# Layer 0 of a graph and feed-forward network: the adjacency product as two float32r products instead of one float32 product

## The chip, the cores and the metric

The kernel runs on one core of one Trainium2 chip. The metric is the time of one execution on the device, in microseconds (us); lower is better. Times given as a median come from runs without a profile. Everything said about where time goes comes from one further execution, which the hardware profiler recorded.

## The reference

There are 32 graphs of 512 nodes with 256 features. Layer 0 is a graph convolution and a feed-forward block, each added to its input after a layer norm; layer 1 is a graph attention and a slice mixer and is not touched by the change. The graph convolution, which the change concerns, is:

```python
a = adj.astype(x.dtype)                       # [32, 512, 512], ones and zeros
h = jnp.einsum('bnf,fu->bnu', x, W_msg)       # messages; x is the normed input
msg_sum = jnp.einsum('bij,biu->bju', a, h)    # sum over the neighbours
deg = jnp.sum(a, axis=1)
messages = jnp.where(deg[..., None] > 0, msg_sum / jnp.maximum(deg, 1.0)[..., None], 0.0)
out = jnp.einsum('bnf,fu->bnu', x, W_upd) + messages + bias
return jax.nn.relu(out)
```

The feed-forward block has two dense branches of 1024 columns (a gelu and a gate) and a tropical branch, the maximum over features of `x + Wt`, followed by piecewise linear functions; the branches are mixed and multiplied by `Wd`. All arithmetic is in float32.

## The kernel before

`layer0_sorted` does layer 0. A graph has 512 rows, four tiles of 128. The graph convolutions run graph by graph. The feed-forward runs over 32 groups of 512 rows that have been put in another order, so that rows needing many lookups in the tropical branch share a tile; the graphs are ordered in four segments of eight.

The convolution of a graph has two generators. `conv_in` loads x and the adjacency (`adji`, int32), casts the adjacency to floating point on GpSimd (line 392), norms x and transposes it to `x1T` (`layer_norm_T`, line 33), and computes the messages `h` (line 403) in two PSUM tiles `ph`, each copied to SBUF by ScalarE (line 405). Column 256 of `h` is set to one by a GpSimd memset (line 397), so that the product with the adjacency yields the degree as well. `conv_out` computes x times `W_upd` (`pu`, line 421), adds the bias into `u` (line 424), and multiplies adjacency by messages (`pm`, line 430): for each of four row tiles, four products of 128 rows are accumulated over 257 columns. VectorE divides by the degree and adds (lines 433 to 435), applies the relu and the residual into `keep` (line 438), norms the result again (lines 441 to 452), looks for its eight greatest values (lines 455 to 457), and ScalarE counts values above a bound (line 460). `rows_of` receives `keep` by DMA. `put_in_order` sorts a segment when its eight graphs are done.

The feed-forward has `sums`, which gathers rows and table entries by indirect DMA on GpSimd's queue (lines 549, 560 and 591) and takes maxima on VectorE (line 594), `mixed`, which does the two dense products (`clsp` and `gatep`, line 619), their activations on ScalarE (line 621), transposes of the tropical values (`tz`, line 626) and the piecewise functions and mixing on VectorE (`acc`, lines 633 to 637), and `down`, which multiplies by `wd` (`po`, line 648) and adds the result into the rows (line 650).

These are generators, woven in a fixed ratio: first the first segment's convolutions with the preparation of the weights (`features`), then the feed-forward groups with the remaining convolutions, and after the last convolution with the beginning of layer 1. The engines' instruction orders are then set by a planner, which places instructions by estimated times and by priority within the order in which they were written, so a change of an operation can move its neighbours. [...]

Buffers: the tag `mm` is a pair of PSUM tiles that `ph`, `pu`, `pm` and `po` use in turn. In SBUF the pool `sa` holds the convolution's tiles; `h` has one buffer, so the memset of the next graph's `h` waits until the last `pm` of this one has read it. The tag `ln_xn` holds normed tiles, in three buffers.

Of the kernel before, what the change touches and what calls it, by code (L numbers as in the profile page):

```python
# [7 lines left out]

F32 = mybir.dt.float32
I32 = mybir.dt.int32  # L10
BF16 = mybir.dt.bfloat16
U32 = mybir.dt.uint32
# [6 lines left out]
P = 128  # L19
N = 512  # L20
D = 256
NT = N // P
# [10 lines left out]
def layer_norm_T(nc, sb, ps, ident, eps, x, xnT, name, kept=None, pool=False):  # L33


    mv = sb.tile([P, NT, 2], F32, tag="ln_mv", name=f"mv{name}", bufs=2)
    for t in range(NT):
        st = sb.tile([P, 6], F32, tag="ln_st", name=f"st{name}_{t}", bufs=4)
        nc.vector.bn_stats(st, x[:, t, :])
        nc.vector.bn_aggr(mv[:, t, :], st)  # L40
    rs = sb.tile([P, NT], F32, tag="ln_rs", name=f"rs{name}", bufs=2)
    if pool:
        deviation(nc, rs, mv[:, :, 1], eps)
        shift = sb.tile([P, NT], F32, tag="ln_shift", name=f"shift{name}", bufs=2)
        nc.vector.scalar_tensor_tensor(shift, mv[:, :, 0], -1.0, rs, ALU.mult, ALU.mult)
    else:
        nc.scalar.activation(rs, mv[:, :, 1], AF.Sqrt, bias=eps[:, 0:1])
        nc.vector.reciprocal(rs, rs)
    pt = [ps.tile([P, NT, P], F32, tag="tp", name=f"lnp{name}_{c}") for c in range(DC)]
    for t in range(NT):  # L50
        if kept is None:
            xn = sb.tile([P, D], F32, tag="ln_xn", name=f"xn{name}_{t}", bufs=3)
        else:
            xn = kept[:, t, :]
        if pool:
            nc.scalar.activation(xn, x[:, t, :], AF.Identity, bias=shift[:, t : t + 1], scale=rs[:, t : t + 1])
        else:
            nc.vector.tensor_scalar(xn, x[:, t, :], mv[:, t, 0:1], rs[:, t : t + 1], ALU.subtract, ALU.mult)
        for c in range(DC):
            nc.tensor.transpose(pt[c][:, t, :], xn[:, c * P : (c + 1) * P], ident)  # L60
    for c in range(DC):
        nc.scalar.copy(xnT[:, c, :], pt[c].rearrange("p t n -> p (t n)"))
# [34 lines left out]
def layer0_sorted(tc, ident, eps, x, adj, w, x2s, ranks, over, following):  # L97
# [29 lines left out]
    with ExitStack() as ctx:  # L127
# [30 lines left out]
        for i, cap in enumerate(CAPS):  # L158
            if i == 0 or cap != CAPS[i - 1]:
                nc.gpsimd.memset(limits[:, i:], 2.0 * cap + 1.0 - D)  # L160
        count_to = cst.tile([P, P], I32, tag="count_to", name="count_to")
        nc.gpsimd.iota(count_to, pattern=[[1, P]], base=0, channel_multiplier=0)
        upto = cst.tile([P, P], BF16, tag="upto", name="upto")
        nc.vector.tensor_copy(upto, count_to)
        nc.gpsimd.iota(count_to[:, 0:1], pattern=[[0, 1]], base=0, channel_multiplier=1)
        own_part = cst.tile([P, 1], F32, tag="own_part", name="own_part")
        nc.vector.tensor_copy(own_part, count_to[:, 0:1])

        CT = NC * ST
        below = cst.tile([P, CT // P, CT], BF16, tag="below", name="below")  # L170
# [213 lines left out]
        def conv_in(b):  # L384

            xg = sa.tile([P, NT, D], F32, tag="x", name=f"x{b}")
            nc.sync.dma_start(xg, x[b].rearrange("(t p) d -> p t d", p=P))
            a = sa.tile([P, NT, N], F32, tag="adj", name=f"adj{b}", bufs=2)
            for t in range(NT):
                ai = sa.tile([P, N], I32, tag="adji", name=f"adji{b}_{t}", bufs=2)  # L390
                nc.sync.dma_start(ai, adj[b, t * P : (t + 1) * P, :])
                nc.gpsimd.tensor_copy(a[:, t, :], ai)
            x1T = sa.tile([P, DC, N], F32, tag="x1T", name=f"x1T{b}", bufs=2)
            layer_norm_T(nc, sa, ps, ident, eps, xg, x1T, f"a{b}", pool=True)
            yield
            h = sa.tile([P, NT, D + 1], F32, tag="h", name=f"h{b}", bufs=1)
            nc.gpsimd.memset(h[:, :, D : D + 1], 1.0)
            for t0 in range(0, NT, 2):
                ph = ps.tile([P, 2, D], F32, tag="mm", name=f"ph{b}_{t0}")
                for i in range(2):  # L400
                    t = t0 + i
                    for c in range(DC):
                        nc.tensor.matmul(ph[:, i, :], x1T[:, c, t * P : (t + 1) * P], w_msg[:, c, :],
                                         start=c == 0, stop=c == DC - 1)
                nc.scalar.copy(h[:, t0 : t0 + 2, :D], ph)  # L405
            held[b] = xg, a, x1T, h
            yield

        def conv_out(b, counts):


            xg, a, x1T, h = held.pop(b)
            keep = sa.tile([P, NT, RW], F32, tag="keep", name=f"keep{b}")
            mv = sa.tile([P, NT, 2], F32, tag="mv", name=f"mv{b}")
            for t0 in range(0, NT, 2):
                two = slice(t0, t0 + 2)
                pu = ps.tile([P, 2, D], F32, tag="mm", name=f"pu{b}_{t0}")
                for k in range(2):
                    t = t0 + k
                    for c in range(DC):  # L420
                        nc.tensor.matmul(pu[:, k, :], x1T[:, c, t * P : (t + 1) * P], w_upd[:, c, :],
                                         start=c == 0, stop=c == DC - 1)
                u = sa.tile([P, 2, D], F32, tag="upd", name=f"u{b}_{t0}", bufs=1)
                nc.vector.tensor_add(u, pu, bias.unsqueeze(1).to_broadcast([P, 2, D]))
                deg = sa.tile([P, 2], F32, tag="deg", name=f"deg{b}_{t0}")
                for k in range(2):
                    t = t0 + k
                    pm = ps.tile([P, N], F32, tag="mm", name=f"pm{b}_{t}")
                    for i in range(NT):
                        nc.tensor.matmul(pm[:, : D + 1], a[:, i, t * P : (t + 1) * P], h[:, i, :],  # L430
                                         start=i == 0, stop=i == NT - 1)

                    nc.vector.tensor_scalar_max(deg[:, k : k + 1], pm[:, D : D + 1], 1.0)
                    nc.vector.reciprocal(deg[:, k : k + 1], deg[:, k : k + 1])
                    nc.vector.scalar_tensor_tensor(u[:, k, :], pm[:, :D], deg[:, k : k + 1], u[:, k, :],  # L435
                                                   ALU.mult, ALU.add)
                    yield
                nc.vector.scalar_tensor_tensor(keep[:, two, :D], u, 0.0, xg[:, two, :], ALU.max, ALU.add)
                for t in range(t0, t0 + 2):
                    st = sa.tile([P, 6], F32, tag="ln_st", name=f"stb{b}_{t}", bufs=4)  # L440
                    nc.vector.bn_stats(st, keep[:, t, :D])
                    nc.vector.bn_aggr(mv[:, t, :], st)
            rs = sa.tile([P, NT], F32, tag="ln_rs", name=f"rsb{b}", bufs=2)
            deviation(nc, rs, mv[:, :, 1], eps)
            shift = sa.tile([P, NT], F32, tag="ln_shift", name=f"shiftb{b}", bufs=2)
            nc.vector.scalar_tensor_tensor(shift, mv[:, :, 0], -1.0, rs, ALU.mult, ALU.mult)
            for t in range(NT):
                k, n = keep[:, t, :], b * NT + t
                nc.gpsimd.tensor_copy(k[:, MEAN : MEAN + 1], shift[:, t : t + 1])
                nc.gpsimd.tensor_copy(k[:, MEAN + 1 : MEAN + 2], rs[:, t : t + 1])  # L450
                xn = sa.tile([P, D], F32, tag="ln_xn", name=f"xnb{b}_{t}", bufs=3)
                nc.scalar.activation(xn, k[:, :D], AF.Identity, bias=shift[:, t : t + 1], scale=rs[:, t : t + 1])
                rest = sa.tile([P, D], F32, tag="rest", name=f"rest{n}")
                bound = ends[:, 0, n : n + 1]
                nc.vector.tensor_tensor_reduce(rest, xn, low, -1.0, 3e38, ALU.add, ALU.min, bound)
                nc.vector.max(k[:, VAL : VAL + 8], xn)
                nc.vector.max_index(k[:, IDX : IDX + 8].bitcast(U32), k[:, VAL : VAL + 8], xn)


                nc.scalar.activation(rest, xn, AF.Sign, bias=bound, accum_out=counts[:, t : t + 1])  # L460
                nc.gpsimd.tensor_copy(k[:, COUNT : COUNT + 1], counts[:, t : t + 1])
                nc.gpsimd.tensor_copy(ends[:, 1, n : n + 1], k[:, VAL : VAL + 1])
                if t + 1 < NT:
                    yield
            rows = rows_of[b // SEG].rearrange("(b t p) w -> b p t w", t=NT, p=P)
            nc.sync.dma_start(rows[b % SEG], keep)
            yield
# [1767 lines left out]
```

## Time and profile before

| what | value |
|---|---|
| median of three runs | 4594.69 us (4590.96 to 4598.55) |
| profiled execution, first to last instruction | 4609.8 us |
| TensorE, VectorE, ScalarE, GpSimd busy | 89%, 73%, 50%, 37% of the span |
| first and last `pm` product | 32.1 us and 1875.4 us |
| first and last `clsp` product | 325.9 us and 2483.1 us |
| mean granted TensorE clock | 0.952 of full speed |

The only time known of the profiled execution is its span; it is 15.1 us (0.3%) longer than the median of the runs without a profile, and no time outside it is recorded. A line such as "L430 PE MATMUL pm<-h,adj" names the line of the kernel, the engine (PE is TensorE, PEld its weight loads, DVE VectorE, ACT ScalarE, POOL GpSimd, SP the queue that issues most DMAs), the operation, and the tiles written and read. Recorded ends of matmuls are modelled, and a record's length includes a drain that the next one overlaps; so the distance between starts, not the length, is what a matmul costs in a row of them. The idle time of an engine is put down to whatever ended it last.

### The profile page before, as it was taken

Reading aid. Unit: us, or ns where it says so; the run is one execution under the profiler, and the core shown is the slowest. Engines: PE = TensorE matmul, PEld = TensorE weight load, DVE = VectorE, ACT = ScalarE, POOL = GpSimd, SP = SyncE. Lnnn points to the kernel's source line nnn. Section 1 sums busy time; section 2 is a strip of 40 time slices with the busy share of each in tenths; the row PEclk is TensorE's granted clock in tenths of the full one; section 3 lists DMA queues with packets and bytes.
Section 4 is the critical chain, followed back from the end, with each engine's and each line's share of the span. In section 5 each row is a group of like instructions: output and inputs, shape, how many; then the busy total and the mean of one; then the engine's idle time right before and its main releaser. Section 6 shows DMA issues by size and latency. Waiting matters only on the chain.

```text
span 4609.8 us, 56079 instructions
## 1 busy us (share of the span) xinstructions
PE 4083.4 (89%) x19287; PEld 2519.8 (55%) x19287; DVE 3357.7 (73%) x6944; ACT 2291.2 (50%) x4756; POOL 1726.9 (37%) x2036
## 2 busy tenths in 40 slices
PE   5767898989989899879897999999999999999997
PEld 4544555656556566545554355555555555555555
DVE  6668777877788877776675777767777777777763
ACT  2344565545655555545564444545444455454433
POOL 2356544654537444353332332222323333222220
PEclk8888999999999999998998999999999999999998
DMA  5556533654437543374431111111111111111100
GB/s 131 162 162 203 172 122 120 202 180 139 141 95 226 168 133 126 97 254 143 137 115 48 53 47 56 54 40 46 46 49 56 56 53 56 46 56 56 40 14 15
DMA packets 235100, 474.09 MB, mean 103 GB/s; under 512 B 38299, under 2 KB 114075, under 8 KB 234804
## 3 DMA queue, kind: packets, MB, share of 16 engines
q0 software_dynamic: 80256, 282.38, 19.1%
q1 hardware_dynamic: 154548, 188.02, 13.3%
q8 instruction: 154, 2.52, 0.2%
q14 instruction: 142, 1.16, 0.1%
HBM read 413.16 MB, written 57.16 MB: 102 GB/s over the span
## 4 chain that ended last, share of the span: by engine, by line
PE 33%; DVE 30%; DMA 11%; POOL 11%; issue 10%; ACT 5%; SPq 0%; DVEq 0%; POOLq 0%; ACTq 0%
DVE att L1209 5%; PE clsp L619 4%; PE gatep L619 4%; PE avp L1242 3%; PE pm L430 3%; DVE acc L633 3%; DMA rows<-table,xs 2%; PE po L648 2%; DVE sw L1332 2%; DVE best L594 2%; PE yTp L1342 2%; DMA rows<-table,tops 2%; DVE sw L1337 2%; PE adp L1249 2%; DVE sst L1335 2%
## 5 line engine op out<-in xcount | busy, mean ns | idle before, releaser
L619 PE MATMUL clsp<-xnT,wc 128*128 128x512 f32 x1024 | 522.8, 629 | 74.0 <-ACT cls L621 57.5
L619 PE MATMUL gatep<-xnT,wg 128*128 128x512 f32 x1024 | 501.6, 608 | 6.8 <-ACT gate L621 5.9
L648 PE MATMUL po<-wd,acc 128*128 128x256 f32 x2048 | 455.1, 382 | 4.9 <-ACT h L405 3.0
L1209 DVE SCALAR_TENSOR_TENSOR att<-own,other,mask 128x512 f32<-128x512 f32 x512 | 392.1, 790 | 75.4 <-DMA own<-ownd 75.4
L648 PEld LDWEIGHTS po<-wd,acc 128*128 128x128 f32 x2048 | 390.5, 192 | 71.5 <-issue 13.0
L430 PE MATMUL pm<-h,adj 128*128 128x257 f32 x1024 | 292.4, 431 | 121.5 <-DVE u L435 46.9
L633 DVE SCALAR_TENSOR_TENSOR acc<-past,fld,acc 128x512 f32<-128x512 f32 x448 | 347.6, 778 | 57.9 <-ACT past L632 47.6
L594 DVE SCALAR_TENSOR_TENSOR best<-rows,xs,best 128x1024 f32<-128x1024 f32 x212 | 274.2, 1296 | 152.6 <-ACT best L588 90.1
L628 ACT ACTIVATE acc<-tz,fld 128x512 f32<-128x512 f32 x256 | 198.6, 776 | 283.6 <-PE tz L626 283.5
L591 POOL DMA_INDIRECT rows<-table,xs x212 | 254.4, 1200 | 218.0 <-DVE best L594 159.5
L619 PEld LDWEIGHTS gatep<-xnT,wg 128*128 128x128 f32 x1024 | 197.5, 196 | 251.6 <-issue 206.3
L632 ACT ACTIVATE past<-tz,fld 128x512 f32<-128x512 f32 x448 | 290.6, 691 | 79.2 <-DVE acc L633 78.8
L619 PEld LDWEIGHTS clsp<-xnT,wc 128*128 128x128 f32 x1024 | 187.6, 201 | 224.5 <-issue 121.2
L430 PEld LDWEIGHTS pm<-h,adj 128*128 128x128 f32 x1024 | 210.2, 216 | 181.4 <-issue 103.0
L1242 PE MATMUL avp<-att,hv 128*64 128x512 f32 x1024 | 304.8, 617 | 2.3 <-DVE att L1209 2.3
L1342 PE MATMUL yTp<-sw,x 128*128 128x512 f32 x512 | 256.2, 636 | 56.9 <-DVE sw L1337 54.0
L621 ACT ACTIVATE cls<-clsp,fld 128x512 f32<-128x512 f32 x256 | 175.1, 684 | 205.5 <-PE clsp L619 97.3
L1295 POOL TENSOR_TENSOR mu<-mu,eps 128x16 f32<-128x16 f32 x32 | 112.9, 3527 | 381.1 <-DVE mu L1294 381.0
L1330 PE MATMUL lgp<-wsl,x4T 128*128 128x512 f32 x512 | 244.3, 611 | 11.0 <-ACT sw L1331 3.7
L1150 POOL DMA_INDIRECT x<-x2s,ranks x128 | 136.2, 1064 | 296.8 <-DVE att L1209 133.1
L621 ACT ACTIVATE gate<-gatep,fld 128x512 f32<-128x512 f32 x256 | 175.3, 685 | 141.4 <-PE gatep L619 113.3
L549 POOL DMA_INDIRECT xs<-rows_of,order x128 | 145.1, 1133 | 228.7 <-DVE acc L633 62.6
(598 smaller groups left out, 8944.3 us busy)
## 6 DMA issues: line engine op xcount, KB each, us to landing
adji<-in_adj SPq DMA_DIRECT2D x128, 256.0 KB
ai<-in_adj SPq DMA_DIRECT2D x128, 256.0 KB
own<-ownd SPq DMA_DIRECT2D x128, 256.0 KB
rows_of<-keep SPq DMA_DIRECT2D x32, 550.0 KB
x<-in_x SPq DMA_DIRECT2D x32, 512.0 KB
x2s<-xs SPq DMA_DIRECT2D x32, 512.0 KB
out<-x SPq DMA_DIRECT2D x32, 512.0 KB
rows<-table,xs POOLq DMA_INDIRECT x212
```

The source lines that it names most:

```text
L430: nc.tensor.matmul(pm[:, : D + 1], a[:, i, t * P : (t + 1) * P], h[:, i, :], start=i == 0, stop=i == NT - 1)
L591: nc.gpsimd.indirect_dma_start(out=row, out_offset=None, in_=table, in_offset=bass.IndirectOffsetOnAxis(ap=idxs[:, k : k + 1].bitcast(U32) ...
L594: nc.vector.scalar_tensor_tensor(m, row, vals[:, k : k + 1], m, ALU.add, ALU.max)
L619: nc.tensor.matmul(pf, wf[:, c, f * P : (f + 1) * P], xnT[:, c, :], start=c == 0, stop=c == DC - 1)
L621: nc.scalar.activation(o, pf, fn, bias=fld[:, f, bf : bf + 1], scale=1.0 if fn == AF.Gelu else 0.5)
L632: nc.scalar.activation(r, z, AF.Relu, bias=fld[:, f, AT + b : AT + b + 1])
L633: nc.vector.scalar_tensor_tensor(y, r, fld[:, f, CH + b : CH + b + 1], y, ALU.mult, ALU.add)
L648: nc.tensor.matmul(po[:, i, :], acc[f][:, t * P : (t + 1) * P], wd[:, f, :], start=f == 0, stop=f == FC - 1)
L1209: nc.vector.scalar_tensor_tensor(e, own[h], other[:, j, h : h + 1], mask[:, j, :], ALU.max, ALU.mult)
L1242: nc.tensor.matmul(pv[q][k * HO : (k + 1) * HO, :], hv[:, j, h, :HO], weighed[b, h, j], start=j == 0, stop=j == NT - 1)
L1330: nc.tensor.matmul(pf, xnT[:, c, t * P : (t + 1) * P], wsl[:, c, :], start=c == 0, stop=c == DC - 1)
L1342: nc.tensor.matmul(py, xn[:, t, c * P : (c + 1) * P], sw[:, t, :], start=t == 0, stop=t == NT - 1)
```

## The change

The product of adjacency and messages is done in float32r instead of float32, twice: once with the messages as ScalarE rounds them on writing a float32r tile (`high`), and once with what the rounding left (`low_half`), which VectorE computes by a subtraction from the PSUM tile. Both are accumulated in the same PSUM tile. The messages tile `h` grows from 257 to 514 columns: 256 of the high half, two of ones, 256 of the low half. The adjacency is cast to float32r.

The rest makes room in SBUF for the larger tile. `u` is no longer a tile of its own but the first 256 columns of `keep`; the tile `rest`, whose elements nobody reads, becomes bf16; the tag `ln_xn` gets two buffers instead of three; and `count_to`, used only at the start, is given back after use, by a pool on the side where the convolution's pool is then placed.

```diff
     for t in range(NT):
         if kept is None:
-            xn = sb.tile([P, D], F32, tag="ln_xn", name=f"xn{name}_{t}", bufs=3)
+            xn = sb.tile([P, D], F32, tag="ln_xn", name=f"xn{name}_{t}", bufs=2 if pool else 3)
...
-        count_to = cst.tile([P, P], I32, tag="count_to", name="count_to")
-        nc.gpsimd.iota(count_to, pattern=[[1, P]], base=0, channel_multiplier=0)
         upto = cst.tile([P, P], BF16, tag="upto", name="upto")
...
+        with tc.tile_pool(name="count", bufs=1, side="right") as counting:
+            count_to = counting.tile([P, P], I32, tag="count_to", name="count_to")
+            nc.gpsimd.iota(count_to, pattern=[[1, P]], base=0, channel_multiplier=0)
+            nc.vector.tensor_copy(upto, count_to)
...
-            a = sa.tile([P, NT, N], F32, tag="adj", name=f"adj{b}", bufs=2)
+            a = sa.tile([P, NT, N], F32R, tag="adj", name=f"adj{b}", bufs=2)
...
-            h = sa.tile([P, NT, D + 1], F32, tag="h", name=f"h{b}", bufs=1)
-            nc.gpsimd.memset(h[:, :, D : D + 1], 1.0)
+            h = sa.tile([P, NT, 2 * D + 2], F32R, tag="h", name=f"h{b}", bufs=1)
+            nc.gpsimd.memset(h[:, :, D : D + 2].bitcast(F32), 1.0)
...
-                nc.scalar.copy(h[:, t0 : t0 + 2, :D], ph)
+                high, low_half = h[:, t0 : t0 + 2, :D], h[:, t0 : t0 + 2, D + 2 :]
+                nc.scalar.copy(high, ph)
+                nc.vector.tensor_sub(low_half, ph, high.bitcast(F32))
...
-                u = sa.tile([P, 2, D], F32, tag="upd", name=f"u{b}_{t0}", bufs=1)
+                u = keep[:, two, :D]
...
                     for i in range(NT):
-                        nc.tensor.matmul(pm[:, : D + 1], a[:, i, t * P : (t + 1) * P], h[:, i, :],
-                                         start=i == 0, stop=i == NT - 1)
+                        for c0, c1 in ((0, D + 2), (D + 2, 2 * D + 2)):
+                            nc.tensor.matmul(pm[:, : c1 - c0], a[:, i, t * P : (t + 1) * P], h[:, i, c0:c1],
+                                             start=i + c0 == 0, stop=i + 1 == NT and c0 > 0)
...
-                xn = sa.tile([P, D], F32, tag="ln_xn", name=f"xnb{b}_{t}", bufs=3)
+                xn = sa.tile([P, D], F32, tag="ln_xn", name=f"xnb{b}_{t}", bufs=2)
...
-                rest = sa.tile([P, D], F32, tag="rest", name=f"rest{n}")
+                rest = sa.tile([P, D], BF16, tag="rest", name=f"rest{n}")
```

More of the change, by code (lines that the diff above doesn't have):

```diff
@@ L9 @@
 F32 = mybir.dt.float32
+F32R = mybir.dt.float32r
 I32 = mybir.dt.int32
@@ L160, in layer0_sorted @@
                 nc.gpsimd.memset(limits[:, i:], 2.0 * cap + 1.0 - D)
-        count_to = cst.tile([P, P], I32, tag="count_to", name="count_to")
-        nc.gpsimd.iota(count_to, pattern=[[1, P]], base=0, channel_multiplier=0)
         upto = cst.tile([P, P], BF16, tag="upto", name="upto")
-        nc.vector.tensor_copy(upto, count_to)
-        nc.gpsimd.iota(count_to[:, 0:1], pattern=[[0, 1]], base=0, channel_multiplier=1)
         own_part = cst.tile([P, 1], F32, tag="own_part", name="own_part")
-        nc.vector.tensor_copy(own_part, count_to[:, 0:1])
+        with tc.tile_pool(name="count", bufs=1, side="right") as counting:
+            count_to = counting.tile([P, P], I32, tag="count_to", name="count_to")
+            nc.gpsimd.iota(count_to, pattern=[[1, P]], base=0, channel_multiplier=0)
+            nc.vector.tensor_copy(upto, count_to)
+            nc.gpsimd.iota(count_to[:, 0:1], pattern=[[0, 1]], base=0, channel_multiplier=1)
+            nc.vector.tensor_copy(own_part, count_to[:, 0:1])
         CT = NC * ST
```

## The prediction

> **What bounds the kernel now.** I read the page's busy shares first, then the busy time by stretch, then the chain for the part that the change touches, then the waits and durations around line 430, the product of adjacency and messages.
>
> The page, sections 1, 4 and 5 (busy time and share; the chain by engine; the group: count, busy us, mean ns, idle time before it):
> ```profile
> PE 4083.4 (89%) x19287; PEld 2519.8 (55%) x19287; DVE 3357.7 (73%) x6944; ACT 2291.2 (50%) x4756; POOL 1726.9 (37%) x2036
> ...
> PE 33%; DVE 30%; DMA 11%; POOL 11%; issue 10%; ACT 5%; SPq 0%; DVEq 0%; POOLq 0%; ACTq 0%
> ...
> L430 PE MATMUL pm<-h,adj 128*128 128x257 f32 x1024 | 292.4, 431 | 121.5 <-DVE u L435 46.9
> ```
> TensorE is the busiest engine, yet only a third of the chain is its own: it and VectorE take turns. The 512 products of line 430 leave 1024 records, so one f32 product is two of them, and 121.5 us of TensorE idleness stands in front of this line alone.
>
> Busy time by stretch. From 326 us, where the feed-forward's products begin, to 1880 us, where the last graph convolution ends, both are woven together:
> ```profile
> core 0: us, PE busy (x) PEld busy (x) DVE busy (x) ACT busy (x) POOL busy (x), PEclk, DMA share, GB/s
> 0.00:326.00 326.00, 211.40 (x876) 165.13 (x877) 209.59 (x758) 112.71 (x239) 114.63 (x325) 0.84 0.50 146
> 326.00:1880.00 1554.00, 1393.36 (x5232) 915.21 (x5231) 1223.77 (x2398) 851.16 (x1465) 796.55 (x1047) 0.96 0.49 156
> ```
> TensorE is busy 90% and VectorE 79% there, each waiting for the other. The head is bound by neither.
>
> The chain by line, from 0 to 1880 us:
> ```profile
> by line: issue 13.7%; PE pm L430 6.7%; PE clsp L619 5.5%; PE gatep L619 5.3%; DVE acc L633 4.6%; DVE best L594 4.2%; DMA rows<-table,xs 3.9%; DMA rows<-table,tops 3.1%; DMA adji<-in_adj 2.9%; POOL rows L591 2.1%; DMA xs<-rows_of,order 2.0%;
> ```
> What TensorE waited for from 326 to 1880 us (total us, times, longest):
> ```profile
> PE pm L430 <- DVE u L435: 38.5, 13, 6.5
> PE pm L430 <- DVE xs L650: 37.4, 15, 5.3
> ```
> Line 430 is the largest named piece: 6.7% of 1880 is 126 us. The waits are for the two PSUM buffers of tag `mm`, which lines 403, 421, 430 and 648 share and VectorE mostly empties.
>
> Durations (min/median/max ns):
> ```profile
> L430 PEld LDWEIGHTS pm<-h,adj x1024: 186/190/338, 31.9 to 1875.1; 128*128 128x128 f32 x171
> L430 PE MATMUL pm<-h,adj x1024: 377/381/797, 32.1 to 1875.4; 128*128 128x257 f32 x171
> L626 PEld LDWEIGHTS tz<-ident,best x1024: 137/141/231, 292.0 to 2485.5; 128*128 128x128 f32 x171
> L626 PE MATMUL tz<-ident,best x1024: 271/273/476, 292.0 to 2485.6; 128*128 128x128 f32 x171
> L491 PE MATMUL rankp<-below,total x12: 325/326/527, 256.7 to 1897.2; 128*128 128x384 bf16 x12
> L650 DVE TENSOR_TENSOR xs<-xs,po x64: 648/681/690, 416.6 to 2499.9; 128x512 f32<-128x512 f32 x64
> L424 DVE TENSOR_TENSOR u<-pu,bias x64: 650/677/692, 32.3 to 1869.0; 128x512 f32<-128x512 f32 x64
> ```
> A record has about 166 ns of drain that the next one overlaps: clsp's 512 columns have a median of 592 ns and po's 256 columns 379, so a column costs (592-379)/256 = 0.83 ns. The bf16 row costs (326-166)/384 = 0.42. An f32 record is thus two passes of 0.42, an f32 product four.
>
> [...] The trace shows 190 ns and 141 ns for f32, but four f32 transposes, each with new weights, take 0.60 us in all, so (600-273)/3 = 109 ns apart[...].
>
> **The change, part by part.**
>
> 1. *The product.* 512 four-pass products of 257 columns become 1024 of 258 or 256. Now a `pm` tile is 8 records 0.217 us apart, 1.74 us (the chain's "pm x8" pieces say 1.72 to 1.76). At one pass, each new product streams 256 × 0.42 = 0.107 us, say 0.11, and its weight load fits under it at the transposes' pace: 8 × 0.11 = 0.88 us. Saved 0.86 × 128 tiles = **110 us of TensorE**, 76 of it after 326 us (704 of the 1024 records). Bounds: if the load's 190 ns set the pace, 8 × 0.19 = 1.52 us, 28 us saved; if a column takes two passes, as the f32 transposes do ((273-166)/128 = 0.84 ns), 8 × 0.217 = 1.74 us, nothing saved. I take one pass[...].
>
> 2. *On the path.* 126 us of pm is on the chain; half of it is 63 us. That is a ceiling if nothing else is as long, since a chain nearly as late takes over.
>
> 3. *The low half.* 64 new subtractions of 128x512 from PSUM at 0.68 us: **44 us more VectorE**, 30 of it after 326 us (1224 to 1254). VectorE's chain share over busy share is 30/73 = 0.41, so 18 us on the path. It waits for ACT's copy of line 405 (573 ns); behind it on VectorE stand the feed-forward's `acc` and `best` steps. pm now waits for it instead of for the copy.
>
> 4. *The PSUM buffer of ph.* It is freed after copy and subtraction instead of copy alone (today 3.3 us of waiting at pm). VectorE's evictions cost TensorE 37.4/64 = 0.58 us each at line 650 and, over the whole span, 46.9/128 = 0.37 at line 435, so 64 × 0.37 to 0.58 = 24 to 37 us of TensorE waiting. It is partly the same delay as in 3; I add 4 us, with 0 and 15 as bounds.
>
> 5. *Room.* `ln_xn` goes from three buffers to two: ACT's third normalised tile waits for the search of the first (line 457), with the feed-forward's evictions queued behind it on ACT. The built order sets a sign step (line 460) between them more often, so most of the wait was there already: 0 to 10 us, I take 2. `u` in `keep`'s place removes 64 tiles of a single buffer (TensorE waited 33.4 us for line 424 in all, mostly for its PSUM): 0 to -5, taken as 0. `rest` in bf16, the f32r copy, cast and memset keep count and element number (0.41, 0.57 and 0.62 us; the memset 0.10 us): 0, within 3 us either way.
>
> 6. *The head.* `count_to` moves to the side where the convolution's tiles lie, and these reuse its place. On SP's queue three 1 MB weight loads now stand before the first `x` and adjacency; on POOL the first cast follows the masks of `below` instead of standing among them. The first x landed at 10.3 us; 3 MB at the 121 GB/s of the first 140 us are 25 us at most, shared. The weight chain (`both`, line 191, at 17.1 us) starts earlier. -5 to +15, I take 3.
>
> Sum: -63 + 18 + 4 + 2 + 3 = **-36 us**. POOL's memset of h waits 171.5 us for pm, with gathers queued behind it; some of that shrinks too and offsets the chain that takes over in 2. I round to -35. The profiled execution's span, 4609.8 us, is 15 us above the median of 4594.7, and no time outside it is shown; so it becomes about 4575, and the median **4560 us**.
>
> **Rivals.**
> - *TensorE is the whole bound* of the weave: all 76 us there plus part of the head's 34 go, less little: 4594.7 - 85 = 4510. For it: 90% busy. Against: pm's share of the weave's own chain is 6.5%, 101 of its 704 × 0.217 = 153 us, and VectorE's 1254 us then nearly equal TensorE's.
> - *VectorE takes it all.* The weave's bound moves to VectorE and the mm ring: 63 less 44 and the upper bounds of 4 and 5 (15) is -4: 4590.
> - *Slower: the four-byte operand takes two cycles a column.* It decides in line 430's TensorE pace: from 0.217 us a product on, eight cost what eight records cost now. Nothing is saved, and 3 to 6 remain: 18 + 4 + 2 + 3 = +27, 4622. For it: the transposes, the only other f32 rows, run so. [...] It is also how the change would fail to do what it says.
>
> **How the numbers follow.** A change under 0.2% (9 us) is what measurement can't tell from none. Main case (-15 to -65): 0.50. TensorE whole bound (to -100): 0.20. VectorE takes it (-12 to +12): 0.12, of which 0.02 is faster, 0.08 the same, 0.02 slower. Two cycles a column: 0.18, of which 0.01 is the same. Faster 0.72, same 0.09, slower 0.19. The range 4510 to 4625 leaves out half of the second case and some of the last.
>
> **What would show it.** Line 430 with 1024 records of about 273 ns each (166 + 107) and 0.11 us apart, VectorE up by 64 rows of 0.68 us, and the weave ending earlier with fewer TensorE and more VectorE microseconds in it. If pm's records last 380 ns, the last rival holds; if they last 273 and the time stays, look for TensorE waiting on the subtraction. A last pm not before 1860 us would make the gain wrong; so would any loss after 2484 us, which nothing here touches.

## The result, and the profile after

The changed kernel takes 4578.2 us (median of five runs, 4570.76 to 4587.94) where the kernel before takes 4594.2 (five runs): a ratio of 0.9957, 95% interval [0.9942, 0.9972], 16 us or 0.43% faster. A repeat on another chip gave 0.9951 [0.9935, 0.9966]. The profiled execution of the changed kernel is one of its five runs, the slowest of them, and that of the kernel before lies 15 us above its median; so the two profiles differ by 23.7 us, where the medians differ by 16.

The page of the changed kernel, sections 1, 4 and 5:
```profile
PE 4011.0 (87%) x19287; PEld 2462.2 (54%) x19287; DVE 3391.6 (74%) x7008; ACT 2296.8 (50%) x4756; POOL 1743.1 (38%) x2036
...
PE 28%; DVE 25%; DMA 7%; POOL 7%; issue 7%; ACT 4%; DVEq 0%; POOLq 0%; SPq 0%; ACTq 0%
...
L436 PE MATMUL pm<-h,adj 128*128 128x258 f32 (+1 forms) x1024 | 180.4, 323 | 111.3 <-DVE keep L441 36.1
```
The product's own busy time fell from 292.4 to 180.4 us, by 112.0 or 38%, with as many records as before. All of TensorE fell from 4083.4 to 4011.0, by 72.4 only. VectorE rose by 34 us, with 64 instructions more. The idle time in front of the product hardly moved (121.5 to 111.3 us). The shares of the chain add up to 78% here, so they can't be set against those of before.

Busy time by stretch, in the same stretches as before: the head, up to the first feed-forward product, and the weave of convolutions and feed-forward.
```profile
core 0: us, PE busy (x) PEld busy (x) DVE busy (x) ACT busy (x) POOL busy (x), PEclk, DMA share, GB/s
0.00:326.00 326.00, 185.44 (x879) 151.24 (x880) 218.13 (x778) 112.76 (x233) 121.28 (x328) 0.79 0.49 149
326.00:1880.00 1554.00, 1366.42 (x5328) 883.29 (x5327) 1267.53 (x2492) 874.23 (x1505) 821.43 (x1069) 0.95 0.49 157
```
In the head TensorE lost 26 us of work, and its granted clock went from 0.84 to 0.79. In the weave VectorE is now busy 82%, TensorE 88%.

Durations of the rows that answer to those shown of before (min/median/max ns), and where the feed-forward's first and last products lie:
```profile
L436 PEld LDWEIGHTS pm<-h,adj x1024: 186/190/338, 37.2 to 1846.3; 128*128 128x128 f32 x171
L436 PE MATMUL pm<-h,adj x1024: 276/284/776, 37.2 to 1846.4; 128*128 128x258 f32 x171
L632 PE MATMUL tz<-ident,best x1024: 271/273/477, 296.9 to 2456.1; 128*128 128x128 f32 x171
L625 PE MATMUL clsp<-xnT,wc x1024: 590/592/1222, 326.5 to 2453.6; 128*128 128x512 f32 x171
L410 DVE TENSOR_TENSOR h<-ph,h x64: 650/682/693, 34.4 to 1790.7; 128x512 fp32r<-128x512 f32 x64
```
A float32r product is one record, of 284 ns, where a float32 product was two of 381. With the drain of 166 ns that the prediction worked out, a column costs (284 - 166)/258 = 0.46 ns, near the 0.42 of one pass. The subtraction takes 682 ns. The first `clsp` starts at 326.5 us (325.9 before), so the head ends where it did; the last starts at 2453.6 (2483.1), so the gain lies between the two.

What TensorE waited for in front of `pm` and `po`, 326 to 1880 us:
```profile
PE pm L436 <- DVE xs L656: 32.8, 14, 3.9
PE pm L436 <- DVE keep L441: 28.5, 9, 6.3
...
PE po L654 <- DVE h L410: 7.2, 5, 5.1
```
The old waits for the pair `mm` stay, somewhat shorter (37.4 and 38.5 us before). One on the new subtraction joins them; before, `po` waited 3.0 us there for ScalarE's copy.

### The profile page after: what moved, and what is told of

Same layout as the page of the kernel before. It is cut to its first block, busy times and chain, and to the rows that moved or that the text cites. A ratio compares the mean times of both kernels' runs of the same rounds, so it can differ in the third digit from the quotient of the medians.

```text
span 4586.1 us, 56206 instructions
## 1 busy us (share of the span) xinstructions
PE 4011.0 (87%) x19287; PEld 2462.2 (54%) x19287; DVE 3391.6 (74%) x7008; ACT 2296.8 (50%) x4756; POOL 1743.1 (38%) x2036
## 4 chain that ended last, share of the span: by engine, by line
PE 28%; DVE 25%; DMA 7%; POOL 7%; issue 7%; ACT 4%; DVEq 0%; POOLq 0%; SPq 0%; ACTq 0%
DVE att L1215 4%; PE avp L1248 3%; PE clsp L625 3%; PE gatep L625 3%; DVE acc L639 2%; DMA rows<-table,xs 2%; DVE sw L1338 2%; PE po L654 2%; PE yTp L1348 2%; DVE sw L1343 2%; PE adp L1255 2%; DVE sst L1341 2%; PE oTp L1536 1%; PE xp L1401 1%; PE zp L1394 1%
## 5 line engine op out<-in xcount | busy, mean ns | idle before, releaser
L625 PE MATMUL clsp<-xnT,wc 128*128 128x512 f32 x1024 | 535.7, 643 | 83.8 <-ACT cls L627 53.2
L436 PE MATMUL pm<-h,adj 128*128 128x258 f32 (+1 forms) x1024 | 180.4, 323 | 111.3 <-DVE keep L441 36.1
L555 POOL DMA_INDIRECT xs<-rows_of,order x128 | 154.8, 1209 | 231.9 <-DVE acc L639 99.2
L1568 PE MATMUL outp<-v,swT 128*128 128x256 f32 x1024 | 227.6, 381 | 0.0
```

Source lines behind the costliest of these rows:

```text
L625: nc.tensor.matmul(pf, wf[:, c, f * P : (f + 1) * P], xnT[:, c, :], start=c == 0, stop=c == DC - 1)
L1568: nc.tensor.matmul(po[:, :D], swT[:, k, t * P : (t + 1) * P], v[:, k, :], start=k == 0, stop=k == KC - 1)
```

## The experiments

Theory A: TensorE's and VectorE's microseconds both count, each only for the share that is on the path. Theory B: TensorE's saving counts in full, and VectorE's added work takes it away. Theory C: room, order (the planner's placing of the instructions) or the head cost what the product gained. Each ratio is to runs of the kernel before on the same chip; 0.1% is 4.6 us. In what follows the changed kernel stands at 0.9954, the mean of its two measurements. Most of the kernels below were measured on other chips than it, so a difference to it is one between ratios, and each such difference is uncertain by about 0.2%, or 9 us.

**The subtraction taken out.**
The high half is multiplied a second time in place of the low half, so TensorE has as much to do.
```diff
...
-                nc.vector.tensor_sub(low_half, ph, high.bitcast(F32))
...
-                        for c0, c1 in ((0, D + 2), (D + 2, 2 * D + 2)):
+                        for k2, (c0, c1) in enumerate( ((0, D + 2), (0, D))):
...
```


> The changed kernel without VectorE's subtraction: the high half is multiplied twice, so the low half of the messages is left out and the sums are twice the rounded ones; TensorE's work is as in the changed kernel. Theory A (turn-taking: both engines' time counts by their share on the path): about 18 to 25 us below the changed kernel, near 4557. Theory B (VectorE took the gain): 40 us or more below it, near 4535. Theory C (room, order or the head took the gain): within 6 us of it.

Measured: 4573.23 us, ratio 0.9932 [0.9919, 0.9945]. That is 0.22% or 10 us below the changed kernel, less than A's 18 to 25 and a quarter of B's 40, so neither size was met. The subtraction's 44 us of VectorE didn't swallow the gain: B falls.

**The float32 product with the subtraction kept, and the room changes alone.**
```diff
-            a = sa.tile([P, NT, N], F32R, tag="adj", name=f"adj{b}", bufs=2)
+            a = sa.tile([P, NT, N], F32, tag="adj", name=f"adj{b}", bufs=2)
...
+                        nc.tensor.matmul(pm[:, : D + 1], a[:, i, t * P : (t + 1) * P], h[:, i, : D + 1],
+                                         start=i == 0, stop=i == NT - 1)
...
```
In the first kernel `h` keeps its 514 columns, in float32, and the product doesn't read the low half. In the second `h` goes back to 257 float32 columns, and the subtraction is gone.

> The changed kernel with the single float32 product of before, the room changes and the subtraction kept; the low half is written and not read, so no product waits for it. Theory A: 18 to 25 us above the kernel before, near 4615. Theory B: 40 us above, near 4635. Theory C: above the kernel before by what the room changes alone cost in x3_room, 10 to 20 us.

> Only the room changes: u in keep, rest in bf16, two buffers of ln_xn, count_to given back; float32 product of 257 columns, no subtraction. Theories A and B: within 6 us of the kernel before, 4594. Theory C: 10 to 20 us slower, near 4610.

Measured: 1.0030 [1.0019, 1.0041] with the subtraction, 0.9994 [0.9986, 1.0001] with the room changes alone. Room costs nothing (-3 us, not told from zero), and the head ends at 325.1 us there, so these two parts of C fall. The subtraction on the old product costs 0.36%, 17 us (14 above the kernel before, where A had 18 to 25). From 1.0030 to 0.9954 the product itself brings 0.76%, **35 us**; without a subtraction on either side (0.9994 to 0.9932) it brings 29. The two agree within their uncertainty.

The third part of C, order, stays open. Every kernel is planned anew, and its instructions change places. In the traces up to 2484 us, the coarse weave of the changed kernel is that of before: the first `pm` of each graph comes after the same number of `clsp` products, within 4 of 1024. In detail it isn't: 48% of VectorE's instructions are followed by another one than before, against 23% with the room changes alone and none between two executions of the changed kernel. So each price here, of a product or of a subtraction, includes what the planner made of it, and no run holds the order fixed while the product changes. Of all the experiments, only the one with a single tile `h` keeps the order of the changed kernel.

**The float32r products done twice.**
```diff
-                        for c0, c1 in ((0, D + 2), (D + 2, 2 * D + 2)):
+                        for k2, (c0, c1) in enumerate(2 * ((0, D + 2), (D + 2, 2 * D + 2))):
...
```


> The changed kernel with both float32r products done twice, so sums and degrees are doubled and their ratio stays; TensorE's pm tile goes from about 0.94 us to about 1.9 us, which adds some 120 us of TensorE, and nothing else changes. Theory A: 30 to 50 us above the changed kernel, near 4620. Theory B: within 15 us of it, as VectorE covers it. TensorE as the whole bound: 100 us above, near 4680.

Measured: 1.0042 [1.0029, 1.0054], 41 us above the changed kernel for 1024 more products. Their durations, and TensorE's total on the page of this kernel:
```profile
L436 PE MATMUL pm<-h,adj x2048: 277/283/861, 35.2 to 1887.5; 128*128 128x258 f32 x94, 128*128 128x256 f32 x93
```
```profile
PE 4082.4 (88%) x20311; PEld 2569.2 (56%) x20311; DVE 3394.5 (74%) x7008; ACT 2295.6 (50%) x4756; POOL 1739.8 (38%) x2036
```
At 0.12 us each they are 123 us of TensorE, a third of it on the path, as A has it. TensorE's busy time rose by 71 us only, and the mean granted clock of the profiled execution from 0.943 to 0.957.

**The relu and residual moved to ScalarE and GpSimd.**
```diff
-                nc.vector.scalar_tensor_tensor(keep[:, two, :D], u, 0.0, xg[:, two, :], ALU.max, ALU.add)
+                nc.scalar.activation(keep[:, two, :D], u, AF.Relu)
+                nc.gpsimd.tensor_add(keep[:, two, :D], keep[:, two, :D], xg[:, two, :])
```


> The changed kernel with the relu and residual of keep (64 VectorE steps of 0.68 us) done as a relu on ScalarE and an addition on GpSimd, so VectorE has as many microseconds as before the change. If VectorE's time counts by its share on the path, as x1_nosub and x2_f32_sub say: 11 to 17 us below the changed kernel. Rival: GpSimd's addition (about 1.6 us by the 0.82 us of its 256-column additions) waits for ScalarE with the gathers queued behind it, and the time is 10 us or more above the changed kernel.

Measured: 1.0064 [1.0049, 1.0079], 51 us above the changed kernel. A's price of VectorE time was no use here; the time rose, as the rival had it. Waits of GpSimd in this kernel, 326 to 1880 us, and one of VectorE:
```profile
POOL xs L556 <- DVE acc L640: 64.7, 7, 12.1
...
POOL keep L445 <- ACT keep L444: 27.8, 16, 7.8
```
```profile
DVE stb L448 <- POOL keep L445: 26.3, 19, 2.1
```
The addition waits for ScalarE 16 times, in front of the gathers on the same engine, and the gathers' own wait for `acc` grew from 47.4 us (its line in the changed kernel is 639). VectorE, which was to be relieved, now waits for the addition before it can take the statistics of `keep`. How the 51 us divide between these waits is not shown.

**One tile h for all graphs.**
```diff
-            h = sa.tile([P, NT, 2 * D + 2], F32R, tag="h", name=f"h{b}", bufs=1)
-            nc.gpsimd.memset(h[:, :, D : D + 2].bitcast(F32), 1.0)
+            h = every_h
...
+        every_h = sa.tile([P, NT, 2 * D + 2], F32R, tag="h", name="h", bufs=1)
+        nc.gpsimd.memset(every_h[:, :, D : D + 2].bitcast(F32), 1.0)
...
```


> The changed kernel with one h tile for all graphs, its columns of ones set once; GpSimd no longer waits for the last product of a graph (114 us of its idle time in 23 waits), ScalarE's copy does. If gathers queued behind that wait are on the path: 10 to 25 us below the changed kernel. If GpSimd's waits only change their name: within 6 us of it.

Measured: 0.9956 [0.9941, 0.9970], the changed kernel's own. What became of the wait, from 326 to 1880 us, in the changed kernel and in this one:
```profile
POOL h L400 <- PE pm L436: 64.0, 13, 10.8
```
```profile
POOL adj L394 <- PE pm L435: 59.5, 13, 10.7
```
In the changed kernel the memset waited. Now the next instruction, the cast into the adjacency tile that `pm` still reads, waits instead. GpSimd's 171.5 us of waiting, which the prediction counted on a little, was a wait for something else as well.

**The pm tiles in the other PSUM pair.**
```diff
-                    pm = ps.tile([P, N], F32, tag="mm", name=f"pm{b}_{t}")
+                    pm = ps.tile([P, N], F32, tag="tp", name=f"pm{b}_{t}")
```


> The changed kernel with the pm tiles in the PSUM pair of the convolution's and the rows' transposes instead of the pair mm. If the waits for mm (61 us of TensorE before pm in the weave) are what keeps TensorE's freed time from the path: 15 us or more below the changed kernel, and those waits fall by half. If they are only VectorE being late, which any pair shows: within 8 us of it, with the waits under other names.

Measured: 1.0010 [0.9998, 1.0023], 26 us above the changed kernel. The first waits of TensorE in the weave are now these:
```profile
PE lnpa L61 <- ACT xna L57: 48.8, 23, 16.1
...
PE xsp L579 <- DVE keep L441: 18.8, 10, 4.4
```
```profile
L625 PE MATMUL clsp<-xnT,wc x1024: 590/592/1222, 347.8 to 2483.0; 128*128 128x512 f32 x171
```
The waits in front of `pm` went, and the transposes, which now share their pair with it, wait instead. Most of the loss lies in the head: the first `clsp` starts at 347.8 us, 21 us later than in the changed kernel, and TensorE waits 96.0 us for ScalarE before the transposes `lnpa` there (42.9 in the changed kernel). Neither expectation held. The planner, too, moved more here than in other kernels (60% of VectorE's instructions have another successor than in the changed kernel). This way of splitting the pair made other work late, so the run doesn't tell whether the pair kept part of the saving from the path.

**One product, without and with the subtraction.** Both leave out the low half of the messages, so the sums are of the high half alone.
```diff
-                        for c0, c1 in ((0, D + 2), (D + 2, 2 * D + 2)):
-                            nc.tensor.matmul(pm[:, : c1 - c0], a[:, i, t * P : (t + 1) * P], h[:, i, c0:c1],
-                                             start=i + c0 == 0, stop=i + 1 == NT and c0 > 0)
+                        nc.tensor.matmul(pm[:, : D + 2], a[:, i, t * P : (t + 1) * P], h[:, i, : D + 2],
+                                         start=i == 0, stop=i == NT - 1)
```


> The low half is left out wholly: one float32r product of 258 columns, no subtraction; 512 records fewer, some 55 us of TensorE less than x1_nosub. If TensorE's time counts by a third, as between x4_twice and the changed kernel: 15 to 20 us below x1_nosub. If the return falls off because the granted clock falls and VectorE and the gathers hold the path: within 8 us of x1_nosub, with a mean clock below 0.945.

> The changed kernel without the second product, the subtraction kept: the low half is computed and not added[...]. If TensorE's time returns two thirds here, as x8_high against x1_nosub says: about 40 us below the changed kernel (61 us of TensorE at 0.12 us a product), and 11 to 17 us above x8_high for the subtraction. If x8_high owed its gain to the missing subtraction or the missing wait on it: within 20 us of the changed kernel.

> The changed kernel again, beside the next two on one chip: about 0.43% below the kernel before, as measured first; if the first measurement was off, anything from 0.2% to 0.7% below.

Measured: 0.9837 [0.9819, 0.9855] without, 0.9888 [0.9869, 0.9906] with, and 0.9951 for the changed kernel beside the latter. The kernel without the subtraction lies 44 us below the one with two products and no subtraction, where 15 to 20 or at most 8 had been expected: the return grew. With the subtraction the gain is 30 us by the mean 0.9954, between the two expectations. So the second product costs 30 us (subtraction present) to 44 us (absent) for 61 us of TensorE, and the subtraction costs 23 us here (11 to 17 expected). Where it shows, in the kernel with one product and no subtraction:
```profile
L623 PE MATMUL clsp<-xnT,wc x1024: 590/592/1223, 317.1 to 2389.0; 128*128 128x512 f32 x171
```
The feed-forward of the kernel with one product and no subtraction spans 2071.9 us, against 2127.1 in the changed kernel.

**One product in the kernel before, and nothing else.** The product is as in the last diff, `h` has 258 float32r columns, and the old buffers stay.

> The kernel before with one float32r product of 258 columns and nothing else changed: no second product, no subtraction, no room changes[...]. If the room changes cost nothing: as x8_high, about 1.6% below the kernel before. If they cost or gain: up to 10 us to either side of that.

Measured: 4528.95 us, 0.9833 [0.9814, 0.9851], as with the room changes (0.9837). It is, with the other kernel of one product and no subtraction, the fastest here, and it needs no room. It adds the high half of the messages only, where the change adds both; whether that suffices is a question of accuracy and not of these times.

## Why the prediction was right or wrong, point by point

The forecast was 35 us faster, within a range that holds the result; 16 and 22 us were measured. The direction and the terms were right, the size of one was not.

- **Step 1, the product.** Right in kind. One pass was an assumption of the prediction; the cost of a column (0.46 ns, where a pass of before was worked out as 0.42) bears it out, and the weight loads start 0.12 us apart, as most of the products do. The rival of two cycles a column is excluded by the 284 ns, for it asked for 380. The saving was put too high. Eight products of a tile start (1.22 - 0.28)/7 = 0.134 us apart by the timeline shown in the last section, not 0.11: the second follows the first after 0.22 us, the others after 0.12 (medians of 128 tiles). So a tile takes 1.07 us instead of 0.88, and 128 tiles free 0.67 × 128 = 86 us instead of 110. That the line's busy time fell by 112.0 all the same goes with what the sum left out: some tiles run at a lower clock and free more (before, one at 592 us takes 3.24 us with a mean clock of 0.61, one at 600 us takes 1.91 at full clock).
- **Step 2, the product on the path, is the term that was mis-sized: -63 predicted, -29 to -35 measured** (room alone to no subtraction; float32 with subtraction to changed). Three things take part, each an estimate. The first is the share saved: the sum took half of pm's 126 us on the chain, while the line's busy time fell by 38%, which would be 48 us. The second is the head: of the 126 us, 25 lie before 326 us (7.6% of the chain there), so 9 to 10 of the 48. The first `clsp` came 5 us sooner with the new product where both kernels subtract (331.3 to 326.5 us) and 2 us sooner where neither does (325.1 to 323.4). The third is the clock. What line 430 gave up was partly used elsewhere on TensorE: 112.0 us off, 72.4 us net. The same instructions became longer, as the pages of before and after show for `clsp`:

```profile
L619 PE MATMUL clsp<-xnT,wc 128*128 128x512 f32 x1024 | 522.8, 629 | 74.0 <-ACT cls L621 57.5
```
```profile
L625 PE MATMUL clsp<-xnT,wc 128*128 128x512 f32 x1024 | 535.7, 643 | 83.8 <-ACT cls L627 53.2
```

The mean rose from 629 to 643 ns, with an unchanged median of 592. The mean granted clock fell from 0.952 to 0.943, so the profiled execution lost (1 - 0.943) × 4586 = 261 us of full clock, where it had lost (1 - 0.952) × 4610 = 221. These 40 us more are as much as the rest of TensorE's work grew by. It isn't the one profile: the clock averages 0.953 over 67 runs of the kernel before and 0.946 over 11 of the changed one. Among the runs of the kernel before, on three chips, the time is 2.0 to 2.9 us longer for each 0.001 less of clock, so 0.007 goes with 14 to 20 us. That is a correlation. No kernel changed the clock by itself, so that removing TensorE's work brings its clock down, and that this costs 14 to 20 us, is likely and not shown.

The three together are at least as large as the shortfall of 28 to 34 us. They overlap, and the order of the instructions and the chain that takes over may have a part in it; I can't divide it further.

- **Two prices.** The sum priced VectorE's time by its chain share over its busy share (0.41), and TensorE's by pm's pieces on the chain (63 of 110, 0.57). By the first rule TensorE's rate is 33/89 = 0.37, the 110 us are worth 41, and the sum is -14 us. That this is so near the measured 16 is partly luck, for single terms are off by some us, but the rate is near the 29 to 35 us that the product brought.
- **Steps 3 and 4, the subtraction and its hold on ph.** 22 us predicted, 10 to 23 measured in three pairs (10 with two products, 17 with float32, 23 with one), whose intervals overlap. The 7.2 us of `po` waiting for it is the hold that was named.
- **Steps 5 and 6, room and the head.** 5 us predicted; -3 and not told from zero. `u` in `keep` and the early release took nothing. The first `pm` moved from 32.1 to 37.2 us (36.1 with the room changes alone) without moving the head's end; that the weight loads ahead of x did it is the prediction's reading and wasn't tested.
- **A sign of being wrong.** Any loss after 2484 us was to be one. From the last `clsp` to the end the changed kernel's profile takes 5.8 us longer than that of before (2132.5 and 2126.7 us). The other eleven profiles take 2125 to 2135 us there, whatever the kernel, so this is no more than that stretch varies.
- **Rivals.** TensorE as the whole bound: doubling the products cost 41 us, not 123. VectorE taking it all: without the subtraction the gain is 31 us. (The sum of that rival used 15 us for the upper bounds of steps 4 and 5, which are 15 and 10; with both it gives 4601 us instead of 4590.) Neither holds. A fits best, with rates from a third of TensorE's time (two products against float32 or against four) to a half and 0.7 (one against two). Why the second product weighs more than the halving of the first stays open. The clock fits part of it: without a subtraction it fell from 0.954 to 0.946 (means of all runs) when the float32 product was replaced, and 29 of 109 us of the line's busy time came through; it stayed at 0.946 when the second product went, and 44 of 68 us came through.

## What to carry to other kernels

Where two engines take turns, price removed and added work by one rule, the engine's share of the chain over its share of busy time, then discount it for what comes late next and for a granted clock that may come out lower (a mean of 0.946 here, where it was 0.953). Here 29 to 35 of 112 us of TensorE's busy time came through. Measure added work by experiments that put it on the old and on the new kernel. An edit lets the planner move other instructions, so compare their order too. Before a wait is removed, look whether the next instruction on that engine needs the same event, and before work is moved to a less busy engine, see what is queued behind it there.

## What the runs showed of the hardware

The recorded weight load of a float32r product is 190 ns, as of a float32 record, yet most products of a tile start 0.12 us apart. The timeline of the changed kernel has a tile of eight:
```profile
594.57 1.03 PEld L436 LDWEIGHTS pm<-h,adj 128*128 128x128 f32 x8
594.60 1.22 PE L436 MATMUL pm<-h,adj 128*128 128x258 f32 x8
```
The loads start (1.03 - 0.19)/7 = 0.12 us apart, so their records overlap, and the length of a record is not the pace of these loads. A float32 transpose of 128 columns has nearly the record of a float32r product of 258 (273 and 284 ns): less the estimated drain of 166 ns, a column costs 0.84 ns in the one and 0.46 in the other.

The records of the granted clock hold only the values 1 and 0.5 in the traces of the kernel before and of the changed one; 442 of 4610 us and 520 of 4586 us are at 0.5. The `clsp` records that lie wholly in these stretches have a median of 1061 ns in both traces, the others 592. So the mean of `clsp` moves and its median doesn't. From 140 to 326 us the granted clock was 0.82 in the kernel before, with 129 us of TensorE's work, and 0.74 in the changed one, with 114:
```profile
140.00:326.00 186.00, 128.99 (x552) 101.44 (x553) 119.00 (x385) 72.55 (x154) 79.15 (x189) 0.82 0.51 165
```
```profile
140.00:326.00 186.00, 114.08 (x547) 93.31 (x548) 122.26 (x394) 71.08 (x148) 84.09 (x189) 0.74 0.52 168
```
From 0 to 326 us, the four kernels with 203 to 211 us of TensorE's work (before, room alone, float32 with subtraction, products twice) have a clock of 0.84 to 0.86. The other nine profiles, with 167 to 187 us, have 0.73 to 0.80. Which of the two follows the other isn't shown.
